# Shared experts, projections and output products of a transformer block laid over all steps, and the last sequence's output by chunk

## The chip, the cores and the metric

The kernel runs on one core of one Trainium2 chip. A core has a matrix engine (TensorE, PE in the profile; PEld is its loading of weights), a vector engine (VectorE, DVE), a scalar engine (ScalarE, ACT), GpSimd (POOL) and SyncE (SP), which here issues most of the data transfers. Each engine works through its own queue in order and waits on semaphores that other engines raise. The metric is the device time of one execution in microseconds (us), the median of several.

## The reference

The input `x` is 4 sequences of 1024 tokens with 256 channels, in float32. The reference normalises every token and adds two branches to `x`: an attention block and a mixture of experts.

```python
x = L0_attn_x
xn = _layernorm(x, axis=-1)
x = x + attention(xn, W_qkv, b_qkv, W_out, b_out) + ffn(xn, w_gate, w1_e, w3_e, w2_e, w1_s, w3_s, w2_s)
```

The attention has 16 heads of 16 channels with rotary positions; softmax over all 1024 keys, then an output product with `W_out`. The mixture takes, for each token, 4 of 16 experts (the best 2 of 4 groups, then the best 4 in them), each a gated unit with 128 hidden channels, weighted by the gate; and to every token it adds two *shared experts*, one gated unit with 256 hidden channels:

```python
routed = jnp.einsum('tef,ehf,te->th', g * u, w2_e, combine)
shared = silu(x @ w1_s.T) * (x @ w3_s.T) @ w2_s.T
return (routed + shared).reshape(shape)
```

## The kernel before

Tokens are worked in tiles of 128 rows: 8 tiles a sequence, 32 in all. The attention runs as 256 *steps*: 4 sequences (`b`) by 4 groups of four heads (`g`) by 16 steps (`s`). A step works on one group's exponentials and, one group ahead, on the next group's maxima:

- four score products `ps` (`exp_one`, L1225: keys by 512 queries, 32 rows deep, so that four of them lie in the array beside each other) and their exponentials `es` on ScalarE (L1234);
- four score products `pm` of the next group (`max_one`, L1183) and their row maxima `mx` on VectorE (L1191). The last group of the last sequence (steps 240 to 255) has no such maxima beside it;
- four products `av` of exponentials with values (`av_part`, L1250), added up over eight steps in one bank.

`step` (L1377) writes this order by hand: a *quad* of two `ps` and two `pm`, then the *units* of this step, then a second quad, then `av` of the step before. If the next step has units (`more`), `av` is done whole at the step's end; if not, half of it, and the other half between the next step's quads. All products go into one pool of eight PSUM banks (`banks`, one bank a product of 512 columns); a bank comes free when VectorE or ScalarE has read it. TensorE's order is the program's (`Kit.pe`), and so is SyncE's (`Kit.sp`, L299).

Everything else lies beside the attention as units or as *bits*. A unit is a closure; `pieces(step)` in the main function (L221) lists the units of a step, and `own` (L1345) adds those of the attention: `max_off` (`pmt`, at `s` 2 and 10), `normalise` (`po`, at `s` 3 and 11), the projection of the next sequence (`project_unit`, one tile in every second step of 29 to 43, 93 to 107 and 157 to 171, which gives queries and keys `pqk`, values `pv`, VectorE's bias addition and POOL's rotation), its transposes three steps on (`turn_unit`, `ptr`), and the output products (`finish`: `turn` with the transposes `pf`, then `product` with `py`). A bit is a piece that is issued between the products of a step: one stage of the routing (`advance`), the scattering of rows to experts (`put`, an indirect transfer by POOL, two a step in steps 33 to 96), or the gathering of results (`get`, the same, and `add`, a VectorE addition, two a step from step 171 on).

The shared experts (`shared_block`, L833) work in 16 blocks of 256 tokens. A block has three units: two `first`, each with the gate product and the up product of 128 hidden channels (`ph_s`, L813) and their activation, and one `last`, which multiplies by `w2_s` (`pso`, L862) and adds the result to `xb`, which the first unit loaded (SP) and to which POOL added the output bias. The sum is stored to `acc` in device memory. Their pace is a due count:

```python
    due = min(SHARED[0][1], 1 + (step - SHARED[0][0]) * 3 // 7)      # from step 10, up to 36 units
    due = min(len(shared), SHARED[0][1] + (step - TILES_FROM - PAIRS) * 2 // 5)   # after the tiles
```

From step 98 to step 170 each step has a unit of the routed experts (`pair_of`, L966: `ext`, `ph_r`, `exy`), with weights loaded two steps ahead and gathered rows `xg` loaded in the step before they are turned.

The normalised input, transposed, stands in `xnT`, two buffers for four sequences; `want` and `reload` (L874, L880) bring the later ones back (1 MB each). Attention and mixture meet in `acc`: `fetch_acc` (L1287) loads four tiles of it, `product` (L1313) adds `py`, and a store writes them back; `get` and `add` take a tile of `acc` as `sum`, add the four routed rows and store it, to the output for sequences 0 to 2. For the last sequence the order is turned round: `add` goes to `acc`, and the output products come last, in steps 254 and 255 and in `last_steps` (L1432), where the last half's chain runs: `oT`, the transposes `po`, the reciprocal and product, the transposes `pf`, the products `py`, two additions and the store.

The functions that the change touches, and what calls them:

Of the kernel before, what the change touches and what calls it, by code (L numbers as in the profile page):

```python
# [42 lines left out]
SHARED = ((10, 36),)  # L43
# [6 lines left out]
def kernel(  # L50
# [166 lines left out]
    n_put = NT * TOPK  # L217
    done = {"shared": 0}
    tiles, ex = None, None

    def pieces(step):  # L221
# [5 lines left out]
        due = 0  # L227
        if SHARED[0][0] <= step:
            due = min(SHARED[0][1], 1 + (step - SHARED[0][0]) * 3 // 7)
        if tiles is not None and not tiles:  # L230
            due = min(len(shared), SHARED[0][1] + (step - TILES_FROM - PAIRS) * 2 // 5)
        while done["shared"] < due:
            now.append(shared[done["shared"]])
            done["shared"] += 1
        if step == TILES_FROM:
            tiles = beside.expert_units(ex.enter_context(ex_pool()))
# [46 lines left out]
class Kit:  # L283


    def __init__(self, tc, banks):
# [3 lines left out]
        self.summed = 0  # L290
# [490 lines left out]
class Beside:  # L781
# [51 lines left out]
    def shared_block(self, blk):  # L833
        k, nc = self.k, self.nc
# [3 lines left out]
        def first(c):  # L838
            def run():
# [6 lines left out]
                if at == 0 and c == 0:  # L846
                    self.want(b)
                fs = slice(c * P, (c + 1) * P)
                st["gu"].append(
                    self.hidden(  # L850
                        self.xnT[b][:, :, at : at + SL],
                        [(k.w1s_sb[:, :, fs], k.w3s_sb[:, :, fs])], f"s{blk}_{c}",
                    )
                )
            return run

        def last():
            po = k.bank([P, R, C], f"pso_{blk}")
            for r in range(R):
                for c in range(FS // P):  # L860
                    k.pe(
                        nc.tensor.matmul(  # L862
                            po[:, r, :],
                            lhsT=st["gu"][c][:, r * P : (r + 1) * P],
                            rhs=k.w2s_sb[:, c, :],
# [3 lines left out]
            nc.vector.scalar_tensor_tensor(st["x"], po, 0.5, st["x"], ALU.mult, ALU.add)  # L869
            self.later.append(lambda: k.sp(k.rows(k.acc, blk * R, R), st["x"]))  # L870

        return [first(0), first(1), last]

    def want(self, b):  # L874

        for n in range(1, B):
            if n not in self.back and n <= b + 1:
                self.reload(n)
# [105 lines left out]
    def get(self):  # L984
# [5 lines left out]
        if kk == 0:  # L990
            self.yg = self.rows.tile([P, TOPK, C], F32, name=f"yg_{t}", tag="yg", bufs=3)
# [33 lines left out]
class Attention:  # L1025
# [7 lines left out]
    def __init__(self, ctx, k, wqkv_sb, bqk_sb, bv_sb, wout_sb, cos_sb, sin_sb):  # L1033
# [26 lines left out]
        self.av, self.accs, self.stores = {}, {}, []  # L1060
# [4 lines left out]
    def project_unit(self, b, t):  # L1065
        self.product(b, t)
        self.rotate(b, t)
# [434 lines left out]
```

## Time and profile before

| what | us |
|---|---|
| median of 3 runs | 1421.13 (1420.94 to 1421.87) |
| the profiled execution | 1426.41 |
| its span, first to last instruction | 1424.7 |
| TensorE busy in the span | 1400.7 |
| VectorE busy | 925.4 |
| ScalarE busy | 780.8 |
| GpSimd busy | 423.0 |
| steps 10 to 97 (122.81 to 562.26 in the span) | 439.45 |
| steps 98 to 169, with the routed experts (to 1081.13) | 518.87 |
| steps 170 to 239 (to 1370.43) | 289.30 |
| steps 240 to 255 and the end (to 1424.7) | 54.27 |

Times in the profile are measured from the span's start. A line of the timeline gives start, length, engine, source line, operation, the tile written and the tiles read, the shapes, and how many instructions of that kind stand together. A product in float32 shows as two records, so that a unit with eight records has four products. The end of a record on TensorE is modelled, and four narrow products can lie over each other; the time of a step is therefore read from start to start. A stretch of the busy times gives its length and then, for each engine, the busy us and the number of instructions.

### The profile page before, as it was taken

To read this page: it belongs to the slowest core of one execution; us is meant where nothing else is said; L and a number is where in the kernel's file an instruction comes from. 1 tells how busy PE (TensorE), PEld (TensorE's weight loads), DVE (VectorE), ACT (ScalarE), POOL (GpSimd) and SP (SyncE) were. 2 spreads that over 40 slices of the span, in tenths; PEclk is the share of its full clock that TensorE was granted. 3 is DMA by queue.
4 is the path that set the end of the run, shared out by engine and by line. 5 is a ranking of instruction groups with operands and counts; after the bars stand their busy time and mean duration, and the time that the engine had idled before them with its cause. 6 is when DMAs were issued, how large, how long until landed. Compare 5 with 4: busy or idle time off the path is not lost.

```text
span 1424.7 us, 26637 instructions
## 1 busy us (share of the span) xinstructions
PE 1400.7 (98%) x9878; PEld 683.9 (48%) x9878; DVE 925.4 (65%) x1702; ACT 780.8 (55%) x1586; POOL 423.0 (30%) x498
## 2 busy tenths in 40 slices
PE   7899999999999999999999999999999999999998
PEld 4443344443444344566566665656564344433333
DVE  6878867668766675444555555554445888899941
ACT  4565544455544555555555555554555555566575
POOL 5401503664443445220000000001224444455500
PEclk9899999999999999999999999999999999999999
DMA  5134743523242224446666666665551334333310
GB/s 185 62 124 167 256 169 115 174 75 104 91 139 92 90 78 141 148 149 189 209 209 201 203 197 216 190 208 168 169 152 56 109 119 130 112 108 111 104 39 30
DMA packets 136673, 199.15 MB, mean 140 GB/s; under 512 B 13920, under 2 KB 99040, under 8 KB 136288
## 3 DMA queue, kind: packets, MB, share of 16 engines
q1 hardware_dynamic: 103088, 137.78, 30.7%
q0 software_dynamic: 12288, 33.57, 7.6%
q10 hardware_dynamic: 21168, 26.10, 5.2%
q8 instruction: 78, 1.28, 0.4%
q14 instruction: 51, 0.42, 0.1%
HBM read 124.01 MB, written 79.69 MB: 143 GB/s over the span
## 4 chain that ended last, share of the span: by engine, by line
PE 97%; DVE 1%; ACT 1%; DMA 0%; issue 0%; POOL 0%; ACTq 0%; DVEq 0%
PE pm L1183 22%; PE ps L1225 19%; PE av L1250 19%; PE ph_r L813 9%; PE exy L947 5%; PE ph_s L813 4%; PE pqk L1088 4%; PE ext L938 2%; PE pso L862 2%; PE py L1320 2%; PE ptr L1164 2%; PE pv L1088 2%; PE po L1274 1%; PE pmt L1206 1%; DVE mx L1191 1%; PE pt L472 1%
## 5 line engine op out<-in xcount | busy, mean ns | idle before, releaser
L1234 ACT ACTIVATE es<-ps 128x512 f32<-128x512 f32 x1024 | 554.8, 596 | 412.6 <-PE ps L1225 228.1
L1191 DVE TENSOR_REDUCE mx<-pm 128x1 f32<-128x512 f32 x1024 | 659.5, 683 | 167.0 <-PE pm L1183 103.4
L1183 PE MATMUL pm<-kT,qT 32*128 32x512 f32 x1792 | 523.1, 641 | 1.4 <-ACT kT L1169 1.4
L1225 PE MATMUL ps<-q,kT 32*128 32x512 f32 x1792 | 506.2, 640 | 0.9 <-DVE q L1211 0.8
L1250 PE MATMUL av<-es,vv 128*32 128x512 f32 (+1 forms) x2576 | 287.4, 517 | 0.0
L1225 PEld LDWEIGHTS ps<-q,kT 32*128 32x128 f32 x1792 | 143.3, 183 | 168.0 <-ACT es L1234 85.1
L1183 PEld LDWEIGHTS pm<-kT,qT 32*128 32x128 f32 x1792 | 157.7, 183 | 66.2 <-issue 23.3
L1250 PEld LDWEIGHTS av<-es,vv 128*32 128x32 f32 x2576 | 51.5, 108 | 240.5 <-issue 216.4
L903 POOL DMA_INDIRECT xs<-rows,slot_i x128 | 123.7, 967 | 128.3 <-DVE mx L1191 111.5
L994 POOL DMA_INDIRECT yg<-ys,slot_i x128 | 121.8, 952 | 126.5 <-DVE mx L1191 121.0
L821 DVE SCALAR_TENSOR_TENSOR th_r<-th_r,ph_r 128x256 f32<-128x256 f32 x72 | 30.3, 421 | 195.9 <-ACT th_r L820 195.9
L1128 POOL TENSOR_TENSOR rot<-qk,sin_sb 128x256 f32<-128x256 f32 x56 | 39.5, 726 | 372.5 <-DVE qk L1109 372.0
L813 PE MATMUL ph_r<-xT,w 128*128 128x128 f32 x1152 | 140.5, 275 | 0.5 <-ACT xT L941 0.5
L813 PEld LDWEIGHTS ph_r<-xT,w 128*128 128x128 f32 x1152 | 134.4, 192 | 0.8 <-ACT xT L941 0.7
L1183 PE MATMUL pm<-qkT,qkT 32*128 32x512 f32 x256 | 78.5, 640 | 1.3 <-DVE mx L1191 1.3
L947 PE MATMUL exy<-w,gu_r 128*128 128x256 f32 x288 | 77.3, 391 | 0.0
L1225 PE MATMUL ps<-q,qkT 32*128 32x512 f32 x256 | 75.4, 640 | 0.3 <-DVE gu_s L823 0.3
L820 ACT ACTIVATE th_r<-ph_r 128x256 f32<-128x256 f32 x72 | 27.7, 384 | 81.1 <-PE ph_r L813 81.1
L947 PEld LDWEIGHTS exy<-w,gu_r 128*128 128x128 f32 x288 | 50.0, 190 | 28.7 <-issue 19.7
L1011 DVE SCALAR_TENSOR_TENSOR sum<-yg,wk,sum 128x256 f32<-128x256 f32 x128 | 60.7, 474 | 0.0
L953 ACT ACTIVATE y<-exy 128x512 f32<-128x512 f32 x72 | 43.8, 608 | 17.7 <-PE exy L947 17.4
L1080 POOL MEMSET vv<- 128x128 f32 x4 | 1.3, 318 | 143.6 <-ACT es L1234 143.6
(178 smaller groups left out, 1224.7 us busy)
## 6 DMA issues: line engine op xcount, KB each, us to landing
w<-we SPq DMA_DIRECT2D x144, 384.0 KB
xs<-zero ACTq DMA_DIRECT2D x8, 2304.0 KB
xg<-xs SPq DMA_DIRECT2D x72, 256.0 KB
ys<-y SPq DMA_DIRECT2D x72, 256.0 KB
acc<-acc SPq DMA_DIRECT2D x14, 512.0 KB
xb<-in_x_dram SPq DMA_DIRECT2D x16, 256.0 KB
acc<-xb SPq DMA_DIRECT2D x16, 256.0 KB
we<-in_w_dram ACTq DMA_DIRECT2D x4, 1024.0 KB
```

What stands on the lines that cost most here:

```text
L813: nc.tensor.matmul(ph[:, n, at], lhsT=w[n][:, c, :], rhs=xT[:, c, at], start=(c == 0), stop=(c == NC_ - 1),)
L903: put = nc.gpsimd.indirect_dma_start(out=k.xs, out_offset=bass.IndirectOffsetOnAxis(ap=k.slot_i[:, t, kk : kk + 1], axis=0), in_=self.rows ...
L947: nc.tensor.matmul(py[:, r, :], lhsT=gus[i][:, r * P : (r + 1) * P], rhs=got[i][1][:, r, 2 * NC_ * F :], start=True, stop=True,)
L953: nc.scalar.activation(y, py, AF.Copy, scale=0.5)
L994: get = nc.gpsimd.indirect_dma_start(out=self.yg[:, kk, :], out_offset=None, in_=k.ys, in_offset=bass.IndirectOffsetOnAxis(ap=k.slot_i[:, ...
L1011: nc.vector.scalar_tensor_tensor(sm[:, 0, :], yg[:, kk, :], k.wk[:, t, kk : kk + 1], sm[:, 0, :], ALU.mult, ALU.add)
L1088: nc.tensor.matmul(ps[half][:, :w], lhsT=self.xnT[b][:, c, n0 : n0 + P], rhs=self.wqkv_sb[:, c, half * HALF : half * HALF + w], start=(c = ...
L1183: nc.tensor.matmul(ps, lhsT=self.qT[b, g // 2][rows, g % 2, qt * P : (qt + 1) * P], rhs=self.kT[b, g // 2][rows, g % 2, hf * HALF : (hf + ...
L1191: k.pace = nc.vector.tensor_reduce(out=self.mx_of[b, g, qt // 4][hf][:, qt % 4, j, :], in_=ps, axis=AX.X, op=ALU.max,).ins
L1225: nc.tensor.matmul(ps, lhsT=self.kT[b, g // 2][rows, g % 2, kc * P : (kc + 1) * P], rhs=self.q2[b, g, qh][rows, :], start=True, stop=True,)
L1234: k.last_exp = nc.scalar.activation(e, ps, AF.Exp, scale=DH**-0.5).ins
L1250: nc.tensor.matmul(av[32 * j : 32 * j + 32, cols], lhsT=self.vv[b][:, kc, h * VS : h * VS + 32], rhs=es[j][:, cols], start=(kc == 0), stop ...
```

## The change

Nothing is computed differently, except that sums are added up in another order; the work is cut finer and put into other steps.

- **Shared experts.** A block has six units: for each half of the hidden channels `gate` (product, tanh on ScalarE, VectorE's first operation) and `up` (product and VectorE's second), and for each row tile a `last`. In steps 10 to 97 one unit goes into each step that has nothing else, and further ones where the count is late; 54 units (9 blocks) come ahead of the routed experts instead of 36 old ones (12 blocks). The other 42 follow from step 170 on, to step 230.
- **Projections.** `product` works the queries and keys in its step as before, the values (`pv`) one step later.
- **Output products.** `finish` gives a turn and four products of one tile in five steps that follow each other, with a 256-wide addition each.
- **The last sequence's output** is added up by chunk of 128 channels. Chunk 0, which needs the first two groups of heads only, is turned and multiplied in steps 231 to 238 and kept in `first`, a buffer of `xnT`'s. In steps 244 to 247 four additions bring it together with `acc`. Chunk 1 of the first half of the queries follows in steps 252 to 254; that of the second half stands alone in the new `last_steps`, cut in pairs of tiles with a store each.
- **Loads.** The last sequence's `xnT` is reloaded at step 110, `acc` is fetched at other steps.

```diff
-SHARED = ((10, 36),)
+SHARED_FROM = 10
+SHARED_FIRST = 9
+RELOAD_AT = 110
...
+    k.at_step[RELOAD_AT] = lambda: beside.reload(B - 1)
...
-        due = 0
-        if SHARED[0][0] <= step:
-            due = min(SHARED[0][1], 1 + (step - SHARED[0][0]) * 3 // 7)
-        if tiles is not None and not tiles:
-            due = min(len(shared), SHARED[0][1] + (step - TILES_FROM - PAIRS) * 2 // 5)
-        while done["shared"] < due:
-            now.append(shared[done["shared"]])
+
+        n, first = done["shared"], SHARED_FIRST * len(shared) // (NT * P // SL)
+        if tiles is None and SHARED_FROM <= step < TILES_FROM and n < first:
+            left = TILES_FROM - 1 - step
+            late = n < first - left * (first + 6) // (TILES_FROM - SHARED_FROM)
+        elif tiles is not None and not tiles and n < len(shared):
+
+            m, since = n - first, step - TILES_FROM - PAIRS
+            late = m < since * 4 // 5 if since <= 25 else m < 18 + (since - 25) * 24 // 34 - 4
+        else:
+            late = None
+        if late or late is not None and not now:
+            now.append(shared[n])
             done["shared"] += 1
...
-        def first(c):
+        def half(c, n):
+            ph = k.bank([P, SL], f"ph_s{blk}_{c}_{n}")
+            w = (k.w1s_sb, k.w3s_sb)[n]
+            for i in range(NC_):
+                k.pe(
+                    nc.tensor.matmul(
+                        ph, lhsT=w[:, i, c * P : (c + 1) * P],
+                        rhs=self.xnT[b][:, i, at : at + SL],
+                        start=(i == 0), stop=(i == NC_ - 1),
+                    )
+                )
+            return ph
+
+        def gate(c):
             def run():
...
+                ph = half(c, 0)
+                th = st["th"] = self.ff.tile([P, SL], F32, name=f"th_s{blk}_{c}", tag="th")
+                nc.scalar.activation(th, ph, AF.Tanh, scale=0.5)
+                nc.vector.scalar_tensor_tensor(th, th, 1.0, ph, ALU.add, ALU.mult)
             return run
 
-        def last():
...
+        def up(c):
+            def run():
+                ph = half(c, 1)
+                gu = self.ff.tile([P, SL], F32, name=f"gu_s{blk}_{c}", tag="gu", bufs=3)
+                nc.vector.tensor_tensor(gu, st["th"], ph, ALU.mult)
+                st["gu"].append(gu)
+            return run
...
-            nc.vector.scalar_tensor_tensor(st["x"], po, 0.5, st["x"], ALU.mult, ALU.add)
-            self.later.append(lambda: k.sp(k.rows(k.acc, blk * R, R), st["x"]))
-
-        return [first(0), first(1), last]
+                x = st["x"][:, r, :]
+                nc.vector.scalar_tensor_tensor(x, po, 0.5, x, ALU.mult, ALU.add)
+                if r == R - 1:
+                    self.later.append(store)
+            return run
...
+        return [gate(0), up(0), gate(1), up(1)] + [last(r) for r in range(R)]
...
-            if n not in self.back and n <= b + 1:
+            if n not in self.back and n <= min(b + 1, B - 2):
...
+    def turn_chunk(self, qh, c, tiles=range(4)):
...
+        pt = k.bank([P, n, P], f"pf_{qh}_{c}_{tiles[0]}")
...
+        nc.scalar.copy(self.oc[:, c, tiles[0] : tiles[0] + n, :], pt)
+
+    def add_chunk(self, qh, c, pairs=range(2)):
...
+        acc = self.first[:, qh] if c == 0 else self.accs[B - 1, qh]
+        for pr in pairs:
+            py = k.bank([P, 2, C], f"pyl_{qh}_{c}_{pr}")
+            for i in range(2):
+                k.pe(
+                    nc.tensor.matmul(
+                        py[:, i, :], lhsT=self.oc[:, c, 2 * pr + i, :],
+                        rhs=self.wout_sb[:, c, :], start=True, stop=True,
+                    )
+                )
+            part = acc[:, 2 * pr : 2 * pr + 2, :]
+            if c == 0:
+                nc.scalar.copy(part, py)
+            else:
                 nc.vector.tensor_tensor(part, part, py, ALU.add)
...
         if self.projects(at):
-            out.append(lambda: self.project_unit(*self.projects(at)))
+            b1, t1 = self.projects(at)
+            out.append(lambda: self.product(b1, t1, (0,)))
+            out.append(lambda: self.rotate(b1, t1))
+        if self.projects(at - 1):
+            out.append(lambda: self.product(*self.projects(at - 1), (1,)))
...
+            turn = {(2, 7): (0, 0), (2, 12): (1, 0), (3, 12): (0, 1)}
+            add = {(2, 8): (0, 0, (0,)), (2, 9): (0, 0, (1,)), (2, 13): (1, 0, (0,)),
+                   (2, 14): (1, 0, (1,)), (3, 13): (0, 1, (0,)), (3, 14): (0, 1, (1,))}
...
+        if (b, g) == (B - 1, NG - 1) and 4 <= s < 8:
+
+            qh, pr = divmod(s - 4, 2)
+
+            def early():
+                part = self.accs[b, qh][:, 2 * pr : 2 * pr + 2, :]
+                nc.vector.tensor_tensor(
+                    part, part, self.first[:, qh, 2 * pr : 2 * pr + 2, :], ALU.add
+                )
+
+            bits.append(early)
...
-            if s == (7 if b + 1 < B else 12):
-                self.fetch_acc(b, 0)
-            if s == 15 and b + 1 < B:
-                self.fetch_acc(b, 1)
+        if g == NG - 1 and b + 1 < B and s == 7:
+            self.fetch_acc(b, 0)
+        if g == NG - 1 and b + 1 == B and s in (0, 1):
+            self.fetch_acc(b, s)
+        if g == 0 and b > 0 and s == 3:
+            self.fetch_acc(b - 1, 1)
 
     def last_steps(self):
...
+        oT = self.one.tile([P, HALF], F32, name="oT_last", tag="oT")
+        nc.scalar.copy(oT[:, :SL], self.last_av[:, :SL])
+        nc.vector.tensor_copy(oT[:, SL:], self.last_av[:, SL:])
...
+        for pr in range(2):
+            self.turn_chunk(qh, 1, range(2 * pr, 2 * pr + 2))
+        for pr in range(2):
+            self.add_chunk(qh, 1, (pr,))
             self.stores.pop(0)()
```

## The prediction

> **What bounds the kernel now.** I read the page's busy times first, then the chain that ended last, then TensorE's timeline of single steps, and last the busy times by stretch, cut at step boundaries. (A step starts with its first `ps` product; there are 256.)
>
> ```profile
> PE 1400.7 (98%) x9878; PEld 683.9 (48%) x9878; DVE 925.4 (65%) x1702; ACT 780.8 (55%) x1586; POOL 423.0 (30%) x498
> PE 97%; DVE 1%; ACT 1%; DMA 0%; issue 0%; POOL 0%; ACTq 0%; DVEq 0%
> ```
>
> TensorE carries the path, and the page shows almost no idle time on it. But 98% busy does not say that it works at its best: the four products of a quad lie over each other, and one that starts late still looks busy. So each step has to be priced. Step 185, TensorE alone:
>
> ```profile
> 1149.37 0.69 PE L1225 MATMUL ps<-q,kT 32*128 32x512 f32 x1
> ...
> 1150.44 1.99 PE L862 MATMUL pso<-w2s_sb,gu_s 128*128 128x256 f32 x8
> 1152.37 0.69 PE L1183 MATMUL pm<-kT,qT 32*128 32x512 f32 x1
> ...
> 1153.44 1.06 PE L1250 MATMUL av<-es,vv 128*32 128x512 f32 x8
> 1154.43 0.69 PE L1225 MATMUL ps<-q,kT 32*128 32x512 f32 x1
> ```
>
> From start to start: quad 1.07 us, unit 1.93, quad 1.07, `av` 0.99, together 5.06. Nothing waits. The stretches, each a start and end, its length, then busy us of PE, PEld, DVE, ACT, POOL, the clock and DMA:
>
> ```profile
> 1242.34:1256.44 14.10, 14.10 (x132) 4.73 (x128) 13.44 (x26) 8.69 (x17) 7.57 (x8) 1.00 0.39 114
> 1154.43:1158.42 3.99, 3.99 (x32) 1.47 (x28) 3.56 (x7) 2.39 (x5) 1.89 (x2) 1.00 0.30 89
> 118.62:122.81 4.19, 4.19 (x32) 1.45 (x28) 3.17 (x7) 3.74 (x6) 1.88 (x2) 1.00 0.75 278
> 1167.54:1171.88 4.34, 4.34 (x36) 1.82 (x32) 3.69 (x7) 3.32 (x7) 2.01 (x3) 1.00 0.33 97
> 1149.37:1154.43 5.06, 5.06 (x36) 2.22 (x32) 4.05 (x8) 2.71 (x6) 1.89 (x2) 1.00 0.44 142
> 422.05:432.04 9.99, 8.68 (x45) 4.45 (x41) 4.09 (x8) 4.43 (x9) 2.23 (x3) 0.83 0.12 41
> 326.26:562.26 236.00, 234.35 (x1629) 96.94 (x1625) 160.86 (x277) 121.26 (x232) 112.73 (x118) 0.99 0.32 108
> 1238.58:1337.53 98.95, 98.95 (x844) 34.26 (x841) 93.23 (x176) 59.94 (x112) 51.21 (x54) 1.00 0.37 108
> ```
>
> Four bare steps take 14.10 us: 3.52 each, although two quads and `av` need 2 x 1.07 + 0.99 = 3.13. The 0.39 are lost because a quad takes four of the eight banks and the next must wait until VectorE and ScalarE have emptied the last one. A step with a transpose unit (`pmt` or `po`, 0.5 us) takes 3.99 for the same reason (packed: 3.6). A step with a 1.93 us unit is packed. So **a bare step wastes TensorE, and work put into it costs less than its length**: 1.93 us of work lengthens a bare step by 1.54.
>
> The other bare kind, where half of an `av` is left over from the step before, takes 3.85 to 4.10 (steps 177 and 184 in the timeline: 3.95, 4.10). Steps with more work, from the same timeline: 2.4 us of units 5.45, 2.9 us 5.92, 3.4 us 6.42; from there on each further us of work costs about 0.9. The stretch at 422.05 holds a hole: step 69's units explain 5.92 of its 9.99 us. All engines stand for some 2 us there, then the clock is halved. Step 77 lasts 5.76 instead of about 4.05. These two holes, 4.1 + 1.7 = 5.8 us, are about what the profiled execution (1426.41 us; span 1424.7) has over the median of 1421.13. I take them for this execution's own.
>
> **The price of the new step.** A half unit of the shared experts (`gate`, `up`, or one row tile of `last`) and one tile of an output product are four 256-wide records, half of the eight: 0.96 us. No step of before holds just that. Lower end: step 185 less half its unit, 4.10. Nearest row: step 9, whose bias product has the same four records and one bank, 4.19. Upper end: step 189 (1167.54), with 1.0 us in two banks and two copies on ScalarE, 4.34. I take 4.15 before the expert tiles and 4.20 after them, where VectorE also adds rows (0.47 us, two a step).
>
> **The change, stage by stage.** What each step holds is counted from the order of TensorE's instructions in the changed program; the new order has a unit in nearly every step, so `av` is no longer split.
>
> - Steps 10 to 19 (49.2 us): VectorE works 45.6 us of it on the routing, TensorE 48.0. The table above would give 42.0, but VectorE bounds it; it loses only 0.7 us of work. Gain between 0.7 and 4.3; I take 2, nearer to VectorE's end.
> - Steps 20 to 28 (45.8): 2 x 3.99, 5 x 4.15, the two routing steps as before (4.59, 8.42) = 41.7. Gain 4.1.
> - Steps 29 to 47 (108.5): 3 x 4.15, 8 x 5.06, 5.45, 4 x 5.92, 3 x 6.42 = 101.3. Gain 7.2, of which most is moved work: these steps lose 5.8 us of units, since 9 blocks of the shared experts instead of 12 now come ahead of the expert tiles.
> - Steps 48 to 97 (236.0, less 5.8 of holes = 230.2): 10 x 3.99, 28 x 4.15, 2 x 4.60, 8 x 5.06, 2 x 5.92 = 217.6. Gain 12.6.
> - Steps 98 to 169 (518.9): packed before and after; `pv` moved one step on gives 8.1 + 8.1 for 9.00 + 7.25. Gain 0.9 from the spread `py`.
> - Steps 170 to 203 (157.5): 5 x 3.99, 18 x 4.20, 3 x 4.63, 5 x 5.06, 5.45, 5.92, 6.42 = 152.5. Gain 5.0.
> - Steps 204 to 230 (98.95): 6 x 3.99, 21 x 4.20 = 112.1. Cost 13.2, for 20.2 us of work.
> - Steps 231 to 239 (32.9): 4 x 3.99, 3 x 4.20, 3.77, 3.52 = 35.9. Cost 3.0: the last sequence's chunk 0, four `pyl` tiles and two `pf`. Their copies (0.6 us) find ScalarE 60% busy.
>
> **The end.** TensorE alone, before:
>
> ```profile
> 1407.06 3.72 PE L1320 MATMUL py<-wout_sb,oc 128*128 128x256 f32 x16
> 1410.71 1.92 PE L1250 MATMUL av<-es,vv 128*32 128x512 f32 x16
> ...
> 1416.21 3.29 PE L1320 MATMUL py<-wout_sb,oc 128*128 128x256 f32 x14 [0.24 <-ACT oc L1311]
> ```
>
> From step 252 (1398.58) to the last `av` (1412.63) it is 14.05 us. After: 2.65 (as step 251 with its `po`), twice 3.09 (as step 254), then a quad and exponentials that set the end, 0.7 + 4 x 0.52 + 0.4 = 3.2: 12.0, gain 2.0. From the last `av` to the end it was 12.07. The new chain has a half-wide copy to `oT`, two pairs of transposes with reciprocal and product, one chunk turned in pairs, then 0.96 us of products twice, the second add 0.69: about 5.3, worked out from 0.59 and 0.42 us rows at half width. The store's issue-to-end was 4.45 (1420.25 to 1424.7), of which 1.95 is the transfer of 512 KB; half as much saves 1.0: 3.5. Sum 8.8, gain 3.2. The four early additions (0.69 each) sit in steps 244 to 247, where VectorE did nothing.
>
> **Queues.** SP: the 1 MB reload of the last sequence leaves steps 66 to 68 and goes to step 110, ahead of the expert loads there. It needs about 3 us (393 GB/s in the stretch that holds the earlier one); the DMA engines are 62% busy there and weights are asked for two steps ahead, gathered rows one. Between 0 and 3.1 late once; I take 1. Blocks 9 to 11 move behind the tiles with their loads on SP, 1.27 us additions on POOL and stores; POOL is 52% busy in the stretch at 1238.58 and gets four of them, 5 us in 112: hidden. The loads of `sum` for tiles 28 and 30 stand on SP behind stores of the same rows; the first addition that needs them is one and a half steps (6 us) behind, a store and a load take some 4 us: between 0 and 3, taken as 0. Without that cover VectorE's queue stands, and with it the maxima behind it. Loads of `acc` come two or more steps ahead of their additions: 0.
>
> VectorE is the next bound: 94% in the stretch at 1238.58. It gets 0.42 us more in each of 21 steps, 102 of 112 us: 91%. Splitting 512-wide additions (0.69) into two 256-wide (0.42) costs 0.15 us a time, about 30 times: 4.5 us of VectorE, at most a fifth of it in that stretch, beside TensorE, so taken as 0.
>
> The Trainium skill speaks against that split: "Perfetto Trace Analysis", section Optimizing Scalar/DVE Operations, gives some 125 ns for each further VectorE instruction on PSUM and advises grouping where the engine is saturated. By the page it would be an estimated 3.8 us, by the row 4.5; if all of it lay on the path, the gain would be 16.0 or 15.3 us. No run here shows it on the path.
>
> **Sum.** -2.0 - 4.1 - 7.2 - 12.6 - 0.9 + 1.0 - 5.0 + 13.2 + 3.0 - 5.2 = -19.8 us. Against the profiled execution: 1426.4 - 5.8 - 19.8 = 1400.8; against the median: 1421.1 - 19.8 = 1401.3. I say **1401.5**.
>
> **Rivals.**
> 1. *Half units do not pack.* Every half step takes 4.34, as step 189. That is 37 x 0.19 + 44 x 0.14 = 13 us more: 1415. For it: all rows of about 1 us but step 9 stand there. Against: those use two banks and two copies.
> 2. *The holes are ordinary.* If plain executions have them too and the changed order doesn't: 5.8 less, 1396. For it: a reload runs some 8 us ahead of the first. Against: the median is lower than the profiled time by 5.3.
> 3. *Slower: VectorE stands behind tanh.* In each of the 32 gate steps VectorE's first operation waits for ScalarE's tanh, and the maxima that empty the banks stand behind it. Before, 26 such waits held 32.4 us, 1.25 each. With all of it on the path: 32 x 1.25 = 40 less 20 gained, 1441. It decides from 0.62 us a gate on. Against: the steps with such a wait already stand at 5.06, packed.
> 4. *No change*: half steps at 4.42 use up the gain (82 of them, 0.24 each).
>
> **How the numbers follow.** Forecast 0.62, rival 1 0.20, rival 2 0.07, rival 3 0.07, rival 4 0.04. All half steps at 4.10, the first stage at its best and no reload cost: -10, so 1391.5. Rival 1, with the end a us worse, 1416. The range is 1391 to 1416. A measurement of this kernel tells about 0.2% (2.8 us) from no change. Faster 0.88, same 0.04, slower 0.08.
>
> **What would show it.** In the changed profile: half steps of 4.10 to 4.20 with quads 1.07 apart; steps 48 to 97 near 218 us; steps 204 to 230 near 112; step 255's last `av` some 12 us behind step 252's start and the end 9 us later. Wrong, if quads after a half unit start their last product 0.2 us late, if VectorE's idle time falls to tanh ahead of maxima, or if TensorE waits for gathered rows at steps 110 to 113.

## The result and the profile after

The changed kernel takes 1423.52 us (median of 20 runs, 1421.23 to 1427.4) against 1421.55 us (20 runs, 1420.31 to 1423.71) for the kernel before: ratio 1.0015, 95% interval 1.0009 to 1.0022. The forecast was 1401.5. The profiled execution took 1423.12 us, its span is 1421.2.

The page's busy times and its chain, of the changed kernel:

```profile
PE 1394.3 (98%) x9390; PEld 654.6 (46%) x9390; DVE 928.3 (65%) x1737; ACT 785.5 (55%) x1591; POOL 423.8 (30%) x498
PE 96%; DMA 2%; DVE 1%; ACT 1%; issue 0%; SPq 0%; POOL 0%; ACTq 0%; POOLq 0%; DVEq 0%
```

They look like those of before, but for one entry: the chain now runs through a DMA for 2% of the span, where it had 0. Busy times by stretch say where. The first four are steps 29 to 47, 48 to 97, 204 to 230 and 231 to 239; then come step 205 (a half unit) and steps 19 and 237 alone. Columns as before: start and end, length, busy us of PE, PEld, DVE, ACT and POOL, clock, DMA.

```profile
219.28:322.12 102.84, 102.84 (x644) 42.33 (x640) 76.04 (x132) 56.41 (x123) 63.85 (x64) 1.00 0.29 95
322.12:541.41 219.29, 219.29 (x1461) 81.49 (x1457) 158.44 (x281) 119.73 (x228) 110.04 (x116) 1.00 0.31 103
1214.11:1327.12 113.01, 113.01 (x760) 40.27 (x756) 102.37 (x196) 62.40 (x118) 54.82 (x57) 1.00 0.37 108
1327.12:1371.07 43.95, 40.39 (x260) 13.98 (x256) 30.73 (x56) 22.95 (x43) 8.50 (x9) 0.92 0.26 77
1218.37:1222.57 4.20, 4.20 (x33) 1.46 (x29) 3.70 (x8) 2.17 (x5) 1.89 (x2) 1.00 0.44 136
166.47:175.74 9.27, 6.93 (x32) 2.00 (x29) 4.13 (x9) 2.49 (x5) 4.60 (x11) 0.73 0.94 348
1351.50:1361.98 10.48, 6.92 (x33) 1.79 (x29) 4.46 (x8) 2.88 (x6) 0.00 (x0) 0.84 0.34 106
```

The stages gain and cost much as forecast, except where the clock column is below 1.00. By the prediction's prices step 19 should take 3.99 us and takes 9.27; step 237 should take 4.20 and takes 10.48. Those are two new holes. TensorE stands idle for 2.34 and 3.56 us in them, and each time the granted clock then is 0.5 for 6.83 us.

**The hole at step 237**, from the timeline of the changed kernel:

```profile
1350.78 1.83 SPq L309 DMA_DIRECT2D acc<-acc  x2
1356.38 1.29 DVE L1501 TENSOR_TENSOR acc<-acc,first 128x512 f32<-128x512 f32 x2 [4.70 <-DMA acc<-acc]
1357.59 1.28 DVE L1243 TENSOR_REDUCE mx<-pm 128x1 f32<-128x512 f32 x2
1358.33 1.85 PE L1277 MATMUL ps<-q,kT 32*128 32x512 f32 x2 [3.56 <-DVE mx L1243]
1361.98 1.22 PE L1277 MATMUL ps<-q,kT 32*128 32x512 f32 x1
```

Line by line: SP issues the load of `acc`; VectorE has nothing to do for 4.70 us but to wait for it, because the early additions (L1501) are next in its queue; the maxima stand behind them; TensorE has no free bank and waits 3.56 us for the maxima. The last line is step 238, where a score product takes 1.22 us in place of 0.69: the halved clock. The additions belong to steps 244 to 247. They are written there inside `issue_after(exponential)`, but that orders only instructions of the exponential's own engine, ScalarE. In all other groups a hook hangs on a maximum as well, which is on VectorE; in the last group there are no maxima. So nothing held these four in VectorE's queue, and the order put two of them ahead of the first maxima of step 237, one in the middle of that step and one in the middle of step 238.

**The hole at step 19**, same view:

```profile
161.04 0.36 SPq L309 DMA_DIRECT2D acc<-xb  x1
161.50 1.41 SPq L309 DMA_DIRECT2D xb<-in_x_dram  x1
168.73 1.26 POOL L868 TENSOR_TENSOR xb<-xb,bo_sb 128x512 f32<-128x512 f32 x1 [5.50 <-ACT es L1286]
170.84 0.38 DVE L631 TENSOR_TENSOR ge_e<-msk 128x64 f32<-128x64 f32 x1 [2.48 <-POOL rk L633]
171.88 2.07 PE L1277 MATMUL ps<-q,kT 32*128 32x512 f32 x2 [2.34 <-DVE mx L1243]
```

The load of `xb` for block 1 of the shared experts is issued at 161.50, behind block 0's store, and POOL's addition of the bias can start only at 168.73. (The view names an exponential, which was long done; the load is the other thing that the addition needs. It has taken some 7 us by then, where transfers of this tile take 3.0 in the median: from 160 to 171 us ScalarE's queue fills the expert buffer with zeros, and all queues together move 348 GB/s. That the fill is what slows it was not tested.) In POOL's queue the addition stands in the midst of the ranking, so the ranking's `rk` come late; VectorE's comparison waits for `rk`, the maxima stand behind the comparison, and TensorE waits for those. In the kernel before POOL waited 17.10 us for such a load as well, for block 2, but behind the ranking, where nobody needed POOL.

### The profile page after: what moved, and what is told of

It reads as the page before. It is cut to its first block, busy times and chain, and to the rows that moved or that the text cites. A ratio compares the mean times of both kernels' runs of the same rounds, so it can differ in the third digit from the quotient of the medians.

```text
span 1421.2 us, 25729 instructions
## 1 busy us (share of the span) xinstructions
PE 1394.3 (98%) x9390; PEld 654.6 (46%) x9390; DVE 928.3 (65%) x1737; ACT 785.5 (55%) x1591; POOL 423.8 (30%) x498
## 3 DMA queue, kind: packets, MB, share of 16 engines
q8 instruction: 74, 1.21, 0.4%
## 4 chain that ended last, share of the span: by engine, by line
PE 96%; DMA 2%; DVE 1%; ACT 1%; issue 0%; SPq 0%; POOL 0%; ACTq 0%; POOLq 0%; DVEq 0%
PE ps L1277 20%; PE pm L1235 19%; PE av L1302 18%; PE ph_r L823 9%; PE exy L982 5%; PE ph_s L855 5%; PE pqk L1149 4%; PE pso L892 2%; PE pv L1149 2%; PE ext L973 2%; PE ptr L1216 2%; PE py L1373 2%; PE pmt L1258 1%; PE po L1328 1%; DVE mx L1243 1%; DMA wqkv_sb<-in_w_qkv_dram 1%
## 5 line engine op out<-in xcount | busy, mean ns | idle before, releaser
L1277 PE MATMUL ps<-q,kT 32*128 32x512 f32 x1792 | 512.5, 644 | 6.8 <-DVE mx L1243 5.9
L1235 PE MATMUL pm<-kT,qT 32*128 32x512 f32 x1792 | 510.4, 643 | 1.4 <-ACT kT L1221 1.4
L1302 PE MATMUL av<-es,vv 128*32 128x512 f32 (+1 forms) x2088 | 277.4, 600 | 0.0
L1235 PEld LDWEIGHTS pm<-kT,qT 32*128 32x128 f32 x1792 | 146.4, 183 | 64.0 <-DVE mx L1243 28.9
L1302 PEld LDWEIGHTS av<-es,vv 128*32 128x32 f32 x2088 | 42.2, 108 | 196.3 <-issue 172.9
L1235 PE MATMUL pm<-qkT,qkT 32*128 32x512 f32 x256 | 73.4, 640 | 0.0
```

What stands on the lines that cost most here:

```text
L1235: nc.tensor.matmul(ps, lhsT=self.qT[b, g // 2][rows, g % 2, qt * P : (qt + 1) * P], rhs=self.kT[b, g // 2][rows, g % 2, hf * HALF : (hf + ...
L1277: nc.tensor.matmul(ps, lhsT=self.kT[b, g // 2][rows, g % 2, kc * P : (kc + 1) * P], rhs=self.q2[b, g, qh][rows, :], start=True, stop=True,)
L1302: nc.tensor.matmul(av[32 * j : 32 * j + 32, cols], lhsT=self.vv[b][:, kc, h * VS : h * VS + 32], rhs=es[j][:, cols], start=(kc == 0), stop ...
```

## The experiments

**The two holes.** Three edits of the changed kernel and a second profiled execution of the kernel before. The first edit makes each early addition wait for the exponential of its own step:

```diff
-                nc.vector.tensor_tensor(
+                add = nc.vector.tensor_tensor(
                     part, part, self.first[:, qh, 2 * pr : 2 * pr + 2, :], ALU.add
                 )
+                k.paced(add.ins)
```

> The changed kernel, but each of the four early additions (acc += first, L1501) waits for the exponential of its own step, so that VectorE's queue takes them in steps 244 to 247 and not in steps 237 and 238. Theory (the additions stand ahead of maxima and wait for the load of acc, 4.70 us; TensorE stands 3.56 us and then has a granted clock of 0.5 for 6.83 us): steps 237 and 238 go from 10.48 and 5.40 us to 4.20 and 3.77, as steps of the same content elsewhere, and the time falls by 7 to 8.5 us from 1423.5 to 1415 to 1416.5. Rival 1, another wait takes the place (the load of acc, or the copies of chunk 0 on ScalarE, hold the same maxima): under 2 us. Rival 2, this wait belonged to the one profiled execution: the time stays at 1423.5 and the changed kernel's hole is absent from other executions anyway.

The second issues one load sooner, ahead of block 0's store:

```diff
 def gate(c): ...
                 if c == 0:
-                    st["x"] = self.ff.tile([P, R, C], F32, name=f"xb_{blk}", tag="y", bufs=3)
-                    k.sp(st["x"], k.rows(k.xf, blk * R, R))
+                    if blk != 1:
+                        self.fetch_x(blk)
+                    st["x"] = self.xb
 def last(r): ...
+                if blk == 0 and r == 0:
+                    self.fetch_x(1)
                 po = k.bank([P, C], f"pso_{blk}_{r}")
+    def fetch_x(self, blk):
+        self.xb = self.ff.tile([P, R, C], F32, name=f"xb_{blk}", tag="y", bufs=3)
+        self.k.sp(self.xb, self.k.rows(self.k.xf, blk * R, R))
```

> The changed kernel, but the load of x for block 1 of the shared experts (xb) is issued on SP with the first output product of block 0, ahead of block 0's store and not behind it; its addition on POOL stays. Theory (POOL's addition waits 5.50 us for this load in the midst of the ranking, VectorE's comparison waits for POOL, the maxima wait behind it, TensorE stands 2.34 us and is then at half clock for 6.83 us): steps 19 and 20 go from 9.28 and 5.08 us to 3.99 and 4.2 to 4.6, and the time falls by 5.5 to 6.5 us from 1423.5 to 1417 to 1418. Rival 1, the ranking on POOL and VectorE is itself the limit there and the load only what came last: under 2 us. Rival 2, the one profiled execution's own: no change.

The third has both edits:

> Both edits, the tied additions and the earlier load of block 1. Theory: they lie 200 steps apart and add up, -12.5 to -15 us against the changed kernel: 1408.5 to 1411, faster than the kernel before by 10 to 13 us (0.7 to 0.9%). What is then still above the forecast of 1401.5, 7 to 9 us, would be many small terms (half steps at 4.20 rather than 4.15, the end, steps 29 to 32) and no third hole. Rival: with these two waits gone other waits show, and the sum is under 10 us.

And the kernel before, unedited:

> The kernel before once more, for a second profiled execution. If its two holes (step 69, 4.1 us, and step 77, 1.7 us) are that execution's own, steps 69 and 77 take about 5.9 and 4.1 us here and the span is about 1419 us. If they are ordinary, they are there again, the span is near 1424.7, and 5.8 us of the gain in steps 48 to 97 would be real.

| kernel | median us (range, runs) | ratio to before, interval | steps 19, 20 | steps 237, 238 |
|---|---|---|---|---|
| changed | 1423.52 (1421.23 to 1427.4, 20) | 1.0015, 1.0009 to 1.0022 | 9.28, 5.08 | 10.48, 5.40 |
| tied additions | 1417.11 (1415.97 to 1418.6, 9) | 0.9973, 0.9964 to 0.9983 | 9.27, 5.34 | 4.20, 3.77 |
| earlier load | 1419.39 (1416.35 to 1423.02, 12) | 0.9990, 0.9982 to 0.9999 | 4.73, 4.20 | 10.60, 4.59 |
| both | 1410.97 (1409.99 to 1411.93, 5) | 0.9931, 0.9918 to 0.9943 | 4.73, 4.20 | 4.20, 3.77 |

The four additions in the timeline of the kernel with both edits (line numbers are 7 higher there), then its steps 19 and 237 and its stretches 29 to 47, 48 to 97 and 204 to 230 by busy times:

```profile
1370.99 0.69 DVE L1508 TENSOR_TENSOR acc<-acc,first 128x512 f32<-128x512 f32 x1 [3.27 <-ACT es L1293]
1372.95 0.69 DVE L1508 TENSOR_TENSOR acc<-acc,first 128x512 f32<-128x512 f32 x1 [1.27 <-ACT es L1293]
1375.30 0.69 DVE L1508 TENSOR_TENSOR acc<-acc,first 128x512 f32<-128x512 f32 x1 [1.66 <-ACT es L1293]
1377.37 0.69 DVE L1508 TENSOR_TENSOR acc<-acc,first 128x512 f32<-128x512 f32 x1 [1.37 <-ACT es L1293]
```

```profile
167.01:171.74 4.73, 4.73 (x33) 1.77 (x29) 3.88 (x9) 2.50 (x5) 1.86 (x7) 1.00 1.05 379
1346.27:1350.47 4.20, 4.20 (x32) 1.46 (x28) 2.37 (x5) 2.55 (x6) 0.00 (x0) 1.00 0.77 235
...
214.39:317.24 102.85, 102.85 (x645) 42.33 (x641) 76.04 (x132) 56.44 (x123) 63.86 (x64) 1.00 0.29 94
317.24:536.51 219.27, 219.27 (x1461) 81.48 (x1457) 158.36 (x281) 119.76 (x228) 110.27 (x116) 1.00 0.31 104
1208.50:1321.90 113.40, 113.40 (x760) 40.45 (x757) 103.27 (x196) 62.50 (x118) 55.56 (x57) 1.00 0.37 108
```

Each edit takes away its own hole and leaves the other; both steps run at full clock with both. The additions now wait in a queue where nothing stands behind them. Together the edits are worth 12.5 us, at the lower end of what was expected, and the kernel with both beats both others: 0.7% faster than before. The two rivals (another wait takes over; the holes are one execution's own) fall. What does not fit to the last microsecond: singly the edits gained 6.4 and 4.1 us, each less than its expected range and 2 us less than together. By stage of the traces the tie gains 8.1 us in steps 231 to 239 and the earlier load 5.0 in steps 10 to 28. The rest of the tie's shortfall lies where its edit does not reach (that execution took 0.9 us more up to step 9 and 0.5 more in steps 204 to 230). Step 19 came to 4.73 us and not to the 3.99 expected; it takes 4.73 in the kernel before, too. With the hole at step 237 left in, the runs scatter over 6.7 us, without it and the other over 1.9. The clock has a part in that: of the 12 runs with the earlier load, the fastest (1416.35) had a mean granted clock of 0.996 and the two slowest (1423.02 and 1421.76) 0.993 and 0.990. Why that hole is worth more in some executions was not settled.

The kernel before, profiled again, took 1420.52 us with a span of 1418.8. Its steps 48 to 97 by busy times:

```profile
326.51:556.35 229.84, 229.84 (x1628) 95.05 (x1624) 160.72 (x277) 121.13 (x232) 112.66 (x118) 1.00 0.33 110
```

229.84 us in place of 236.00, full clock; step 69 takes 5.89 and step 77 takes 4.10. So the two holes of before were that execution's own, and this second execution is the one to compare stages with.

**What each part of the change is worth without the holes.** Five kernels, each on top of the one with both edits, undo one part. The last sequence's output as before:

```diff
-            turn = {(2, 7): (0, 0), (2, 12): (1, 0), (3, 12): (0, 1)}
-            add = {(2, 8): (0, 0, (0,)), ...}
+        if g == NG - 1 and s == (13 if b + 1 < B else 14):
+            self.parts = self.finish(b, 0)      # last sequence: one turn, one product
...
+        for part in self.finish(b, 1):          # last_steps
+            part()
```

> On top of the kernel with tied additions and the earlier load (1410.97 us): the last sequence's output as in the kernel before, both chunks of a token half in one piece (turn at the last group's step 14, products in step 255 and behind the last av), no early additions, loads of acc at the old places; the spread shares stay. What is left to price is the new ending without its hole. Theory: steps 231 to 239 give back 3.0 us (35.87 to 32.90), the stretch from step 252 to the end takes 4.0 more (17.86 to 20.91, and 5.2 for 4.24 behind the last product): 1411.0 to 1412.5, so the new ending by itself is worth about 1 us and its hole cost eight times that. Rival: the ending is what made the rest possible and its undoing costs 3 us or more, 1414 or above.

Whole units from block 3 on:

```diff
-        return [gate(0), up(0), gate(1), up(1)] + [last(r) for r in range(R)]
+        if blk > 2:
+            return [both(gate(0), up(0)), both(gate(1), up(1)), both(last(0), last(1))]
+        return [gate(0), up(0), gate(1), up(1)] + [last(r) for r in range(R)]
```

> On top of the kernel with tied additions and the earlier load (1410.97 us): from block 3 on the units of the shared experts are whole again, gate with up and both row tiles of the last product in one step, 39 units of 1.93 us in place of 78 of 0.96; the number of blocks ahead of the expert tiles and all else stay. Theory (prices by step, from the rows: bare 3.52, half unit 4.20, whole unit 5.06, 2.9 us of work 5.92): two half steps cost 8.40, a whole and a bare one 8.58; with the units that shared a step with other work counted, steps 29 to 47 fall to 94, 48 to 97 rise to 226.5, 172 to 203 by 3 and 204 to 230 stay: +3 us in all, 1413 to 1416. Rival 1, spreading is what the whole gain came from: +8 us or more. Rival 2, VectorE behind tanh is spared by whole units (one tanh for two products): no loss, 1411 or less.

Twelve blocks ahead of the expert tiles:

```diff
-SHARED_FIRST = 9
+SHARED_FIRST = 12
-            late = m < since * 4 // 5 if since <= 25 else m < 18 + (since - 25) * 24 // 34 - 4
+            late = m < since * 2 // 5
```

> On top of the kernel with tied additions and the earlier load (1410.97 us): twelve blocks of the shared experts ahead of the expert tiles, as in the kernel before, and not nine; half units stay. 18 half units move from bare steps behind the tiles to steps 29 to 97, which have no bare step left. Theory by the prices of steps: steps 29 to 97 +12 to 14 us, steps 172 to 230 -12 to -13.5: between 1410 and 1413. Rival: a unit that comes on top of other work costs its full 0.96 us, +17 against -13.5, 1414.5.

Projections in one step:

```diff
-            out.append(lambda: self.product(b1, t1, (0,)))
+            out.append(lambda: self.product(b1, t1))
-        if self.projects(at - 1):
-            out.append(lambda: self.product(*self.projects(at - 1), (1,)))
```

> On top of the kernel with tied additions and the earlier load (1410.97 us): the projections of a token tile in one step again (pqk and pv together, as in the kernel before), none in the next; all else stays, and the shared experts' units find the same places. Theory by the prices of steps (the steps concerned are packed, whichever of the two carries pv): steps 29 to 47 +0, 48 to 97 +0.9, 98 to 169 +0 to +1.5, 170 to 203 -0.8: 1410.5 to 1412.5. Rival: a step with the whole projection (2.9 us, and two evictions on two engines) holds up the quads' banks, +3 us or more.

Output products in one step:

```diff
-        return [turn] + [lambda i=i: product(i) for i in range(4)]
+        return [turn, all_four]        # all_four: product(0) to product(3)
```

> On top of the kernel with tied additions and the earlier load (1410.97 us): the four products of an output half of sequences 0 to 2 in one step again (3.85 us), not in four steps; the three steps set free take half units of the shared experts, which comes off the steps that held both. Theory by the prices of steps: 48 to 97 +0.6, 98 to 169 +0.9 (the gain forecast there), 172 to 203 +2.9, 204 to 230 -2.0 as fewer units are left: +1.5 to +3 us, 1412.5 to 1414. Rival: in packed steps the place of the products is all the same, +0.5 or less.

Differences to the kernel with both edits, by stage of the profiled executions, in us:

| undone | 29–47 | 48–97 | 98–169 | 170–203 | 204–230 | 231–239 | 252–255 | median of the runs (range) |
|---|---|---|---|---|---|---|---|---|
| new ending | 0.0 | 0.0 | 0.0 | +0.5 | -0.7 | -3.0 | +3.1 | 1411.93 (1410.31 to 1413.29) |
| half units | -6.4 | +7.7 | 0.0 | +3.6 | -1.0 | 0.0 | 0.0 | 1413.84 (1413.22 to 1414.57) |
| blocks behind the tiles | +5.4 | +7.4 | 0.0 | -6.0 | -6.9 | 0.0 | 0.0 | 1412.02 (1409.63 to 1413.44) |
| projections | +0.5 | +1.0 | +0.3 | -0.3 | -0.2 | 0.0 | 0.0 | 1414.21 (1410.91 to 1415.26) |
| output products | 0.0 | +0.5 | 0.0 | +3.3 | -2.8 | 0.0 | 0.0 | 1411.39 (1410.85 to 1415.32) |

Two rows show how closely prices by step carry a stage. With whole units, steps 29 to 47 and 48 to 97 were put at 94 and 226.5, and steps 204 to 230 were to stay at 113.4; the first came out 2.5 us higher, the others within 1 us:

```profile
214.87:311.33 96.46, 96.46 (x613) 37.28 (x609) 74.81 (x124) 55.32 (x120) 62.23 (x62) 1.00 0.29 94
311.33:538.28 226.95, 226.95 (x1516) 89.69 (x1512) 163.35 (x289) 120.79 (x231) 112.25 (x117) 1.00 0.33 111
1213.91:1326.35 112.44, 112.44 (x845) 43.54 (x841) 100.12 (x193) 62.16 (x118) 55.42 (x58) 1.00 0.37 107
```

With twelve blocks ahead, +12 to +14 was expected in steps 29 to 97 and -12 to -13.5 in steps 170 to 230; it is +12.7 and -12.9:

```profile
215.83:324.04 108.21, 108.21 (x672) 47.38 (x668) 79.41 (x139) 56.97 (x125) 65.20 (x65) 1.00 0.35 114
324.04:550.69 226.65, 226.65 (x1505) 86.64 (x1501) 163.89 (x292) 121.31 (x232) 113.03 (x118) 1.00 0.30 100
1069.95:1216.65 146.70, 146.70 (x1001) 54.80 (x997) 125.15 (x240) 84.46 (x165) 68.66 (x72) 1.00 0.38 112
1216.65:1323.14 106.49, 106.49 (x801) 37.22 (x797) 98.15 (x186) 61.26 (x115) 53.60 (x56) 1.00 0.37 108
```

The stages ahead of step 29 and from 240 to 251 are left out. None of these edits reaches the first; steps 10 to 19 differ all the same, by 1.1 us in two of these executions and by 3.4 in one (see the last section). The new ending's undoing does reach the second, and they take 28.43 us with and without it. The stages hold scatter of their own: the kernel of the next paragraph, whose edit lies behind step 255, takes 0.6 us more in steps 170 to 203.

What follows: no part is worth much by itself. Half units bring 3 to 4 us. The projections bring 1.2 by the stages; their median lies above the expected range and is told of in the last section. The output products bring 1.1 by the stages and 0.4 by the medians; both are under the 1.5 to 3 that was expected, and the rival, that in packed steps their place is all the same, is not excluded. The new ending brings about 0.7: the stages of the table are 0.1 shorter without it, but from the last product to the end it takes 4.2 us with it and 5.0 without it, since the last store is shorter; so it paid about 8 us in its hole for a gain of under 1. That fewer blocks stand ahead of the tiles brings nothing that can be told (the stages sum to -0.2 when it is undone): 18 half units cost as much on top of other work as in bare steps behind the tiles. Of these, only the half units' price stands clear of the scatter of five runs; the rest is read from the stages. The five rows add up to some 7 of the 10.5 us that both profiles differ by. The rest has no price of its own: blocks 0 to 2 keep their half units in all of these kernels, and no edit undid steps 10 to 28.

**A copy in two halves.** The new `last_steps` copies half of the last `av` with ScalarE and half with VectorE, into one tile. In the changed kernel the second copy starts when the first ends. This edit, again on top of both, gives each half a tile of its own:

```diff
-        nc.scalar.copy(oT[:, :SL], self.last_av[:, :SL])
-        nc.vector.tensor_copy(oT[:, SL:], self.last_av[:, SL:])
+        nc.scalar.copy(oTs[0][:, :SL], self.last_av[:, :SL])
+        nc.vector.tensor_copy(oTs[1][:, :SL], self.last_av[:, SL:])
```

> On top of the kernel with tied additions and the earlier load (1410.97 us): the last group's av is copied out into two tiles, the half for ScalarE and the half for VectorE, and not into two halves of one tile. Theory (the second copy waits for the first because they share a tile, some 0.4 us): 0.3 to 0.6 us less, 1410.4 to 1410.7, seen in the distance from the last av to the end. Rival: the copies are not what sets the end, no change.

1411.74 us (1410.21 to 1414.95): no change. The timeline of this kernel:

```profile
1399.61 0.37 ACT L1569 COPY oT_last<-av 128x256 f32<-128x256 f32 x1 [1.14 <-PE av L1309]
1400.02 0.42 DVE L1570 COPY oT_last<-av 128x256 f32<-128x256 f32 x1 [5.02 <-ACT oT_last L1569]
1400.04 0.90 PE L1575 MATMUL po_last<-ident,oT_last 128*128 128x128 f32 x4 [0.46 <-ACT oT_last L1569]
1400.50 0.20 PEld L1575 LDWEIGHTS po_last<-ident,oT_last 128*128 128x128 f32 x2 [0.26 <-DVE oT_last L1570]
```

VectorE still waits for ScalarE's copy, so the common target was not the reason: in the program VectorE's wait is on ScalarE's copy, and what the two copies have left in common is the bank of `av` that they read. The Trainium skill, "PSUM — Partial Sum Buffer", section PSUM bank collisions raise a hardware error, asks that two engines never touch one bank and quadrant at once, reads included; that the program serialises the copies agrees with it. No run has the copies at the same time, so that the bank is the reason is argued and not shown. Little was to be had: the weights of TensorE's second pair of transposes (the last line) wait 0.26 us, and the view puts that down to VectorE's copy.

## Why the prediction was wrong

It was wrong by 22 us: 12.5 from two waits that it put at zero, 9.3 from terms that were each a little too good. Forecast and outcome by stage, in us, against the second execution of before (each row rounded by itself):

| stage | forecast | changed kernel | with both edits |
|---|---|---|---|
| steps 10 to 19 | -2.0 | +3.3 | -0.8 |
| 20 to 28 | -4.1 | -2.3 | -3.2 |
| 29 to 47 | -7.2 | -5.7 | -5.7 |
| 48 to 97 | -12.6 | -10.6 | -10.6 |
| 98 to 169, with the reload | +0.1 | +0.4 | +0.4 |
| 170 to 203 | -5.0 | -4.0 | -4.7 |
| 204 to 230 | +13.2 | +14.1 | +14.4 |
| 231 to 239 | +3.0 | +11.1 | +3.0 |
| 240 to the end | -5.2 | -4.2 | -3.8 |
| up to step 9 | 0 | +0.2 | +0.4 |
| sum | -19.8 | +2.3 | -10.5 |

**The step that failed first**: "The four early additions (0.69 each) sit in steps 244 to 247, where VectorE did nothing", with "Loads of `acc` come two or more steps ahead of their additions: 0". The code puts them there; VectorE's queue in the changed program has them seven steps sooner, right behind the load's issue. The load took the 4.70 us that VectorE waited, and what was priced at nothing cost 7.9 us in steps 237 and 238 (15.88 for 7.97). The prediction had named the mechanism, for the loads of `sum` ("VectorE's queue stands, and with it the maxima behind it"), and then looked for it at the wrong load.

**The second**: "1.27 us additions on POOL" were called hidden by POOL's busy share, and only in the stretch at 1238.58. The same additions come in steps 10 to 28, where POOL's queue holds the ranking, on which VectorE depends. A busy share of 30% says nothing on a queue in which one instruction waits for a load. The profile of before had the sign: POOL stood idle for 57.3 us there, 14 times, until such a load of `xb` had landed. That cost 5.4 us in steps 18 to 20 by the trace (the steps take 18.74 us with it and 13.3 without), 6.1 by the medians.

**Terms that were too good.** The half step was taken at 4.15 ahead of the tiles and is 4.20 where nothing else holds it up. Of the 28 such steps in 48 to 97, 26 take 4.20, and the two with an output half's transposes (61 and 69) 4.34; together that is the 1.7 us by which this stage lies above its 217.6. The timeline of step 205 of the changed kernel, first product of each quad and the work between:

```profile
1218.37 0.69 PE L1277 MATMUL ps<-q,kT 32*128 32x512 f32 x1
...
1219.44 1.13 PE L892 MATMUL pso<-w2s_sb,gu_s 128*128 128x256 f32 x4
1220.50 0.69 PE L1235 MATMUL pm<-kT,qT 32*128 32x512 f32 x1
...
1221.57 1.06 PE L1302 MATMUL av<-es,vv 128*32 128x512 f32 x8
1222.57 0.69 PE L1277 MATMUL ps<-q,kT 32*128 32x512 f32 x1
```

1.07 + 1.06 + 1.07 + 1.00 = 4.20: quad, unit, quad, `av`, packed, as the prediction's second reading had it, with 0.10 us more for the unit than half of 1.93. Steps 29 to 47 missed 1.5 us: step 29 took 5.65 for 5.06 and step 32 took 5.86, both among the first steps with projections; VectorE is busy for all of step 29 and for 5.56 us of step 32. Steps 10 to 19 gained 0.8 of the 2. VectorE was said to bound them and is busy there for 41.95 of 48.34 us with both edits (45.6 of 49.2 before), so that its work alone is not the reason; what is was not settled.

Steps 204 to 230 take 113.40 with both edits for the 112.1 forecast. Of the 1.3 us, 1.0 lies in steps 208, 216 and 224 (4.63, 4.63, 4.36), those in which POOL adds the bias for a block: these additions, too, were called hidden. What they do shows in step 186 of two kernels that differ behind step 255 only, the one with two copies (the first two lines) and the one with both edits:

```profile
1129.08 1.27 POOL L869 TENSOR_TENSOR xb<-xb,bo_sb 128x512 f32<-128x512 f32 x1 [3.46 <-ACT es L1293]
1129.12 1.51 DVE L1054 SCALAR_TENSOR_TENSOR sum<-yg,wk,sum 128x256 f32<-128x256 f32 x1
...
1129.49 0.47 DVE L1054 SCALAR_TENSOR_TENSOR sum<-yg,wk,sum 128x256 f32<-128x256 f32 x1
1129.54 1.55 POOL L869 TENSOR_TENSOR xb<-xb,bo_sb 128x512 f32<-128x512 f32 x1 [3.55 <-ACT es L1293]
```

Where POOL starts first, by 0.04 us, VectorE's addition of a row takes 1.51 us for 0.47, and the step 4.51; where VectorE starts first, it takes its 0.47, POOL's addition 1.55 for 1.27, and the step 3.99. In step 208 a small maximum (128 by 16) takes 1.25 us in this way, mostly 0.18. Which engine comes first changes from execution to execution, and the stages from 170 to 230 scatter with it.

The end gained 3.8 of 5.2. From the last `av` on it is 8.7 us where 8.8 was forecast; what failed is the term ahead of it, "a quad and exponentials that set the end", put at 3.2: from the start of step 255 to the last `av` it is 4.4 with both edits (1395.20 to 1399.6). Steps 240 to 251 took 0.3 more.

**What was right.** TensorE stays the bound; half units pack (rival 1's 4.34 is not there); the cost of steps 204 to 230 was within 1.2 us and that of steps 231 to 239 exact but for the hole; the reload at step 110 cost nothing; before's two holes were its own, so rival 2 falls; VectorE behind tanh (rival 3) holds nothing up, since from step 28 on steps with a `gate` alone take 4.20 like those with a `last`, and VectorE's waits for this tanh came to 9.7 us in all, for 32.4 before. The 0.9 us seen for output products in steps 98 to 169 was not there: undoing them moves that stage by 0.0.

## What to carry to other kernels

When an instruction moves, look it up in the order of its own engine's queue and not in the code: a hint that orders one engine's work leaves the others free, and a cheap instruction that waits for a load stops all that is queued behind it. Busy shares can't show that; ask of every moved load and addition who stands behind it. Prices taken step by step from the timeline held to within three per cent of a stage here. But where the matrix engine is the bound, a stall can cost more than its length: the two of 2.34 and 3.56 us cost 5.4 and 7.9, and behind both the granted clock was 0.5 for 6.83 us.

## What the runs showed of the hardware

After each idle time of TensorE of 2.34 us or more in the middle of these executions (2.34 twice, 3.48, 3.56) the granted clock was 0.5 for 6.83 us; after one of 1.31 us, in the first execution of before, for 3.41 us. The trace's record of the clock lets all such stretches begin a whole number of 3.413 us apart: in the changed kernel at 54.69, 170.75 and 1358.58 us, 34.0 and 348.0 times 3.413. The Trainium skill, "TensorE: Matmul & The Clock Gate", section What's actually happening, has such a window of some 3.4 us and a half rate after an idle one; the grid and the lengths agree with it, but idle times well under a window were enough here.

The same idle time need not have the same price. At step 10 TensorE waits 1.21 or 1.22 us in every kernel here, and goes on at full clock, except in the profiled execution with the projections in one step:

```profile
126.59 0.66 PE L1265 MATMUL pmt<-ident,mx 128*128 128x128 f32 x4 [1.21 <-DVE mx L1250]
...
131.39 1.22 PE L1284 MATMUL ps<-q,kT 32*128 32x512 f32 x1
```

and, by busy times, just behind it:

```profile
129.00:136.00 7.00, 7.00 (x29) 2.26 (x28) 4.52 (x17) 1.68 (x3) 0.00 (x0) 0.54 0.79 295
```

Here the clock fell to half for 6.83 us and steps 10 to 19 took 3.4 us longer than with both edits, though nothing of the projections' edit runs there. That execution took 1415.26 us; the same kernel's other runs lie at 1410.91, 1411.56, 1414.21 and 1414.69, in two groups some 3 us apart. Only one of them has a trace, but the mean granted clock is known of each: 0.992 and 0.993 in the two slowest, 0.996 in the two fastest. The run of 1414.21 us had 0.995 and a span of 1411.0, so that more of it than elsewhere lies outside the span (3.2 us, for 1.7 to 2.3). That is why this median is not taken for the price of that part. The slowest runs with whole output products (1415.32) and with two copies (1414.95) had a clock of 0.992, too. Where in these runs the clock fell was not seen.

Nor is the 1.1 us by which steps 10 to 19 are longer with twelve blocks ahead and with whole output products a matter of the clock, which is full there: 1.0 of it lies in step 15, where, with twelve blocks, VectorE's comparisons take 1.36 and 1.19 us beside POOL's ranking, for 0.52 and 0.55 with both edits alone.
